# A graph network kernel: the first layer's preparation reordered, and the second layer's chunk checks moved into the first layer's loop

## The chip, the core and the metric

The kernel runs on one core of a Trainium2 chip. The metric is the device time of one execution in microseconds (us), the median of several runs. Engines are named as in the profile: PE is the matrix engine (its weight loads are listed as PEld), DVE the vector engine, ACT the scalar engine, POOL the GpSimd engine, and SP the engine that only issues DMAs. A small q behind a name (SPq, ACTq, POOLq) means the part of that engine that issues DMAs and waits.

## What is computed

Two message passing layers run over one graph with 6250 nodes of 64 features and 200000 edges. The edges are sorted by target (`dst`). `src` and `dst` are integers, and every edge has 64 features of its own.

```python
h = relu(layernorm(x))
# layer 0: a graph convolution with degree norm
deg = segment_sum(1, dst) + 1; dis = rsqrt(deg)
h0 = h @ W
agg = segment_sum(h0[src] * (dis[src] * dis[dst])[:, None], dst) + h0 * (dis * dis)[:, None]
x = x + (h + gelu(agg + b))
h = relu(layernorm(x))
# layer 1: a message network over [h[src], h[dst], edge_attr]
m = relu(concat(h[src], h[dst], edge_attr) @ mW1 + mb1) @ mW2 + mb2
agg = segment_sum(m, dst)
x = x + relu(concat(agg, h) @ uW1 + ub1) @ uW2 + ub2
```

## The kernel before

The order of PE, DVE, ACT and SP is written out by hand in the first two stages (of POOL too in the first): an engine executes its instructions in the order in which the code issues them. There are three stages one after the other.

**The preparation** (`pre`) loads the node features, `src` and `dst`, and builds what the first layer needs. Its steps are these.
- `runs` holds `dst` as 125 rows of 1600. DVE compares every hundredth target with the blocks' limits, PE counts, and `at_run_i` says in which run of 100 each block of nodes begins. POOL gathers those runs (13 indirect DMAs at L392), and `begin` (L423 to L427) finds in them where each group of four nodes begins (`gstart`).
- POOL gathers 192 targets and 192 sources for each of 13 blocks of groups (`gdst`, then `gsrc`, L451).
- `offsets` turns `gdst` on DVE into offsets in the group. `sums` (65 times on ACT, L473) sums them for the degrees. `keys` (L516 to L558) turns a pair of blocks into the low bits of the sources, which go to DRAM through one of two buffers `lows`, and into `key_a` and `key_b`, which PE transposes (`pk`) and ACT and DVE copy out of PSUM.
- `feature_major` transposes the normed features into `hT` in groups of four tiles (PE, then an ACT copy). From the degrees comes `dis`; `gs_block` (PE `ph` L201, DVE L203) makes the scaled features in seven parts, and two casts on ACT and two subtractions on DVE split each part into three bf16 terms `hs`.
- `dstd` and `srcd` are the second layer's "chunk" edges (119 chunks of 1024 edges, 8 per partition), loaded in pieces of 32 bytes. From `dstd` DVE computes, for the second layer, `base`, `off`, `sel`, `nsel`, `ends` and a few checks (`third`, `want`, `more`). `dstb` and `srcb` are the edges of 22 "sections" (28 per partition), from which come `bits`, `hib` and checks of the same kind.
- A table of +1 and -1 (`nbit`, `own`, `table`) is built on DVE at the start.

**The first layer** is a loop over 196 "quads" (49 tiles of sources with four quads each). In a quad PE recodes low bits into a one-hot form (`bank` L893), ACT applies a threshold (`cl` L896), DVE makes one-hot keys (`cka` eight times, `ckb` four times, L907), PE multiplies the two into counts (`pc` L913), ACT or DVE copies the counts out (`a` L918), and PE multiplies the counts with `hs` (`small` L932). A `cka` or `ckb` lies in one of a ring of buffers: DVE can make the next only when PE has finished with the oldest.

```python
ok = cw.tile([P, m], BF16, name=name, bufs=12 if e < 2 else 6)
nc.vector.tensor_scalar(ok, iota_k[:, :m], key[:, col : col + 1], None,
                        op0=ALU.is_equal)
```

Between the quads, by a list of events (`at(n, engine, f)`), 22 sections of the second layer's edges are put into place. A section `s` begins at quad `s * 190 / 22`: DVE `mark` in the same quad, PE `before` (28 matmuls, L783) one quad later, ACT `carry` (L787) two later, then DVE `scan` (L791) three, `place` (L798 to L806) four and `codes` (L814 to L821) five quads later. Edge features are loaded by SP, transposed and multiplied on PE (`turn`, `term`), copied by ACT, and POOL scatters 28 x 128 rows per section to DRAM (L851). Every seven tiles a group of nodes is finished (`node_steps`).

**The second layer** then works through 119 chunks and 22 sections, and takes over half of the time. The diff does not touch its code.

Of the kernel before, what the change touches and what calls it, by code (L numbers as in the profile page):

```python
# [22 lines left out]
J = 8  # L23
# [14 lines left out]
def kernel(  # L38
# [103 lines left out]
    def tail(v):  # L142
        return v[TAIL:E].rearrange("(p j) -> p j", j=J)
# [40 lines left out]
    upper_b = kp.tile([P, P], BF16, name="upper_b")  # L184

# [21 lines left out]
    with tc.tile_pool(name="pre", bufs=1) as pre, \  # L207
# [10 lines left out]
        dstd = pre.tile([P, CD, J], I32, name="dstd")  # L218
        nc.sync.dma_start(dstd[:, : CD - 1, :], edges(dst, 0, CD - 1, EB))
        nc.sync.dma_start(dstd[:, CD - 1, :], tail(dst))  # L220
# [35 lines left out]

        ident = const.tile([P, P], F32, name="ident")
# [18 lines left out]
        top = pre.tile([P, P], F32, name="top")  # L276
        nc.gpsimd.memset(top, 0.0)
        nc.gpsimd.memset(top[:1], 1.0)
        want = pre.tile([P, NS + CD], F32, name="want")
# [8 lines left out]
        for i in range(2):  # L288
            t = pre.tile([P, 2, KS, GS], BF16, name=f"lows{i}")
            nc.gpsimd.memset(t[:, :, KS - 1, :], 1.0)  # L290
            lows.append(t)
# [19 lines left out]
        ident_h = const.tile([P, P], F16, name="ident_h")  # L311
# [22 lines left out]


        nbit = pre.tile([P, KS, P], I32, name="nbit")
        for k in range(KS - 1):
            nc.vector.tensor_scalar(nbit[:, k, :], num, k, 1, op0=ALU.arith_shift_right,
                                    op1=ALU.bitwise_and)
        nc.vector.tensor_tensor(nbit[:, KS - 1, :], num, ti[:, 1:2].to_broadcast([P, P]),  # L340
                                ALU.arith_shift_right)
        nc.vector.tensor_scalar(nbit[:, KS - 1, :], nbit[:, KS - 1, :], 1, None,
                                op0=ALU.bitwise_and)
        own = pre.tile([P, 2, P], F32, name="own")
        nc.vector.tensor_reduce(own[:, 0, :], nbit[:, : KS - 1, :].rearrange("p k n -> p n k"),
                                AX.X, ALU.add)
        nc.vector.tensor_scalar(tf[:, 3:], tf[:, :1], float(KS - 1), None, op0=ALU.is_equal)
        nc.vector.tensor_scalar(own[:, 0, :], own[:, 0, :], -2.0, float(KS), op0=ALU.mult,
                                op1=ALU.add)
        nc.vector.tensor_scalar(own[:, 0, :], own[:, 0, :], tf[:, 3:], None, op0=ALU.mult)  # L350
        nc.vector.tensor_scalar(own[:, 1, :], nbit[:, KS - 1, :], 2.0, -1.0, op0=ALU.mult,
                                op1=ALU.add)
        nc.vector.tensor_add(own[:, 0, :], own[:, 0, :], own[:, 1, :])
        pair = pre.tile([P, PW], F32, name="pair")
        nc.vector.tensor_scalar(pair, iota[:, :PW], tf[:, 1:2], None, op0=ALU.is_equal)
        nc.vector.tensor_tensor(table, own[:, :1, :].to_broadcast([P, PW, P]),
                                pair[:, :, None].to_broadcast([P, PW, P]), ALU.mult)

# [32 lines left out]
        for b in range(NB):  # L391
# [5 lines left out]
        lead = pre.tile([P, NS + CD], F32, name="lead")  # L397
        nc.vector.tensor_copy(lead[:, :NS], dstb[:, :, 0])
        nc.vector.tensor_copy(lead[:, NS:], dstd[:, :, 0])
        pbase = few(NS + CD)  # L400
        nc.tensor.matmul(pbase, top, lead, start=True, stop=True)
        base = pre.tile([P, NS + CD], F32, name="base")
        nc.vector.tensor_copy(base, pbase)
        nc.vector.tensor_scalar(at_i, base[:1], float(NP - P), 0.0, op0=ALU.min, op1=ALU.max)
        off, offb = dstd.bitcast(F32), dstb.bitcast(F32)
        nc.vector.tensor_tensor(off, dstd, base[:, NS:, None].to_broadcast([P, CD, J]), ALU.subtract)
        nc.vector.tensor_tensor(offb, dstb, base[:, :NS, None].to_broadcast([P, NS, SJ]),
                                ALU.subtract)
        nc.vector.tensor_copy(bits[:, :, :, 1], offb)
        nc.vector.tensor_scalar(bits[:, :, :, 0], srcb, P - 1, None, op0=ALU.bitwise_and)  # L410
        nc.vector.tensor_scalar(srcb, srcb, 7, None, op0=ALU.arith_shift_right)
        nc.vector.tensor_copy(hib, srcb)


# [5 lines left out]
        def begin(b0_, n):  # L420
# [9 lines left out]
        begin(*begins[0])  # L430


        nc.vector.tensor_tensor(sel, off, off[:, :, 0:1].to_broadcast([P, CD, J]), ALU.not_equal)
        third = pre.tile([P, CD, J], BF16, name="third")
        nc.vector.tensor_tensor(third, off, off[:, :, J - 1 : J].to_broadcast([P, CD, J]),
                                ALU.not_equal)
        begin(*begins[1])
        nc.vector.tensor_mul(third, third, sel)
        more = pre.tile([P, 7], F32, name="more")
        nc.vector.tensor_tensor(want, base, want, ALU.is_lt)  # L440
        nc.vector.tensor_reduce(more[:, 5:6], want, AX.X, ALU.max)
        begin(*begins[2])
        nc.vector.tensor_tensor(most, base[:, :NS], most, ALU.is_gt)
        nc.vector.tensor_reduce(more[:, 6:], most, AX.X, ALU.max)
        nc.vector.tensor_reduce(more[:, 4:5], third.rearrange("p c j -> p (c j)"), AX.X, ALU.max)
        begin(*begins[3])
        for b in begins[4:]:
            begin(*b)
# [28 lines left out]
        mean = pre.tile([P, Q], F32, name="mean")  # L477
        nc.vector.tensor_reduce(mean, xs, AX.X, ALU.add)
        nc.vector.tensor_scalar(mean, mean, 1.0 / D, None, op0=ALU.mult)
        offsets(*pairs[0])  # L480
        sums(*pairs[0])
        xc = pre.tile([P, Q, D], F32, name="xc")
        nc.vector.tensor_tensor(xc, xs, mean[:, :, None].to_broadcast([P, Q, D]), ALU.subtract)
# [28 lines left out]
        def keys(b0_, n):  # L512
# [5 lines left out]
            lo = lows[b0_ // 2 % 2]  # L518
# [27 lines left out]
            for i, to in enumerate((key_a, key_b)):  # L546
# [3 lines left out]
                if i < 1:  # L550
                    nc.scalar.copy(to[:, b0_ * P : (b0_ + n) * P],
                                   pk[:, :n].rearrange("p b g -> p (b g)"))
                else:
                    pkv = pk[:, :n].rearrange("p b (g two) -> p (b g) two", two=2)
                    c = slice(b0_ * P // 2, (b0_ + n) * P // 2)
                    for e in range(2):
                        r = slice(64 * e, 64 * e + 64)
                        nc.vector.tensor_copy(to[r, c], pkv[r, :, e])  # L558

        quads = blocks(4)  # L560
        for q in quads[:4]:
            feature_major(*q)
        sums(*pairs[5])
        keys(*pairs[0])
        for q in quads[4:8]:
            feature_major(*q)
        sums(*pairs[6])
        keys(*pairs[1])
        for q in quads[8:]:
            feature_major(*q)  # L570
# [7 lines left out]
        keys(*pairs[2])  # L578
# [18 lines left out]
        keys(*pairs[3])  # L597

        gs = xc
        for i, (q, n) in enumerate(blocks(8)):  # L600
            s = slice(q, q + n)
            gs_block(psum, gs, q, n)
            nc.scalar.copy(hs[:, s, 0, :], gs[:, s])
            if i < 3:
                keys(*pairs[4 + i])
            nc.vector.tensor_sub(gs[:, s], gs[:, s], hs[:, s, 0, :])
            nc.scalar.copy(hs[:, s, 1, :], gs[:, s])
            if i:
                nc.vector.tensor_sub(hs[:, last, 2, :], gs[:, last], hs[:, last, 1, :])
            last = s  # L610
        nc.vector.tensor_sub(hs[:, last, 2, :], gs[:, last], hs[:, last, 1, :])

        for i, v in enumerate((off.rearrange("p c j -> p (c j)"),
                               offb.rearrange("p s j -> p (s j)"))):
            nc.vector.tensor_reduce(more[:, i : i + 1], v, AX.X, ALU.max)
            nc.vector.tensor_reduce(more[:, 2 + i : 3 + i], v, AX.X, ALU.min)
        nc.vector.tensor_scalar(more[:, :2], more[:, :2], float(P), None, op0=ALU.is_ge)
        nc.vector.tensor_scalar(more[:, 2:4], more[:, 2:4], 0.0, None, op0=ALU.is_lt)
        nc.vector.tensor_reduce(flag[:, NS:], more, AX.X, ALU.max)
        nc.vector.tensor_reduce(nsel, sel, AX.X, ALU.add)  # L620
        for i in range(2):
            nc.vector.tensor_copy(ends[:, i], off[:, :, i * (J - 1)])

        nc.vector.memset(ends[:DDONE, :, CD - 1], -1.0)
# [126 lines left out]
    def section_events(pool, psum, at, pace, placed):  # L751
# [107 lines left out]
        for s in range(NS):  # L859
            o = Section(s)  # L860
            n0 = s * pace
            at(n0, "dve", o.mark)
            at(n0 + 1, "pe", o.before)
            at(n0 + 2, "act", o.carry)
            at(n0 + 3, "dve", o.scan)
            at(n0 + 4, "dve", o.place)
            at(n0 + 5, "dve", o.codes)
            for b in range(Q // 7):
                at(n0 + b, "sp", lambda s=s, b=b: clear(s + 2, b))
            for j0, n in blocks(J, SJ):  # L870
                m = n0 + 3 + j0 * pace / SJ
                for d, engine, f in ((-4, "sp", o.load), (0, "pe", o.turn), (1, "act", o.turned),
                                     (2, "pe", o.term), (3, "act", o.put)):
# [4 lines left out]
    with tc.If(is_bad < 1) as branch:  # L878

        with tc.tile_pool(name="cw", bufs=2) as cw, tc.tile_pool(name="cn", bufs=1) as cn, \  # L880
# [17 lines left out]
            def count(n, i, a, ol):  # L898
                w, q = divmod(n, NQD)
                pc = psum.tile([P, 2, 512], F32, name="pc")  # L900
                for u in range(2):
                    pr = w * PW + q * QP + i + u
                    for e in range(3):
                        key, col, m, name = ((key_a, 2 * pr + e, KA, "cka") if e < 2 else
                                             (key_b, pr, KB, "ckb"))
                        ok = cw.tile([P, m], BF16, name=name, bufs=12 if e < 2 else 6)
# [48 lines left out]

            here, events = [0], {}
# [520 lines left out]
```

## Time and profile before

| | us |
|---|---|
| median of three runs (2473.94 to 2478.30) | 2474.47 |
| the profiled execution | 2476.56 |
| its span from first to last instruction | 2474.80 |
| of it: preparation, up to the first `cb` load | 158 |
| of it: the first layer, up to the second layer's steady work | 945 |
| of it: the second layer | 1372 |

Engine time inside the three stretches (busy us, from the windows view):

| stretch | PE | DVE | ACT | POOL | granted PE clock |
|---|---|---|---|---|---|
| 0 to 158 | 42.8 | 108.1 | 51.7 | 57.8 | 0.80 |
| 158 to 1103 | 845.3 | 798.2 | 728.5 | 693.0 | 0.94 |
| 1103 to 2475 | 1174.9 | 1010.4 | 873.8 | 958.8 | 0.88 |

A group of the profile is a line, an engine and an operation with what it writes and reads; then come the count, the busy time and the mean duration of one in ns, and behind the second bar the time that the engine sat idle just before them and who ended that idle time. A line of the waits view is a waiting engine and line, what it waited for, the total, the number of times, and the longest. A line of the timeline is start, duration, engine, line, operation and shapes, with the idle time before it in brackets. The windows view has, after the stretch, the busy time of PE, PEld, DVE, ACT and POOL, the granted clock of PE as a share of full speed, the DMA share and GB/s.

### The profile page before, as it was taken

What the parts mean: (1) busy time and instruction counts of PE and PEld (TensorE: products, weight loads), DVE (VectorE), ACT (ScalarE), POOL (GpSimd) and SP (SyncE); (2) the same over time, 40 slices, a digit from 0 to 9 for tenths busy, and PEclk for the clock granted to TensorE, in tenths of its full rate; (3) what the DMA queues carried; (4) which work ended last, traced back from release to release, by engine and by line L of the source; (5) the groups of instructions that cost most, each with busy time, mean ns of one, the idle gap of its engine ahead of it and who ended that gap; (6) DMA issues with size and microseconds to landing.
All of it is one profiled execution on the core that took longest, in us unless ns stands there. A gap on an engine that the chain in (4) does not pass through costs nothing.

```text
span 2474.8 us, 50145 instructions
## 1 busy us (share of the span) xinstructions
PE 2062.9 (83%) x17607; PEld 1740.3 (70%) x17607; DVE 1916.7 (77%) x6239; ACT 1653.9 (67%) x3773; POOL 1709.6 (69%) x1676
## 2 busy tenths in 40 slices
PE   0369999998989998858888888888888888888887
PEld 0247777776767776647777777777777778777775
DVE  7678989888887988747768776776677787767875
ACT  0648787877778887746666665665567576656664
POOL 6307777777777777757777777777667677767770
PEclk9769999999999998977889998998889898989997
DMA  9423323332323231133333332233223232322210
GB/s 149 88 68 103 100 95 109 98 105 93 103 90 105 90 120 54 41 82 90 79 75 83 96 84 75 77 79 78 69 76 79 62 85 75 81 72 80 76 50 9
DMA packets 216156, 205.47 MB, mean 83 GB/s; under 512 B 118369, under 2 KB 166369, under 8 KB 215886
## 3 DMA queue, kind: packets, MB, share of 16 engines
q1 hardware_dynamic: 140258, 141.92, 20.6%
q0 software_dynamic: 51840, 57.23, 9.1%
q10 hardware_dynamic: 23788, 2.94, 1.2%
q8 instruction: 143, 2.34, 0.4%
q14 instruction: 127, 1.04, 0.1%
HBM read 133.66 MB, written 68.28 MB: 82 GB/s over the span
## 4 chain that ended last, share of the span: by engine, by line
PE 32%; ACT 13%; DVE 5%; DMA 3%; issue 2%; POOL 2%; SPq 0%; DVEq 0%; ACTq 0%; POOLq 0%
PE duo L1346 9%; PE pz L1328 6%; ACT oh L1320 5%; ACT h L1193 4%; PE pl L1316 3%; PE pp L1179 3%; PE pl L1204 2%; POOL g L746 2%; PE pz L1332 2%; PE mix L1182 2%; ACT hid L1339 1%; DMA g<-table,srcd 1%; PE pe L1160 1%; ACT h L1191 1%; PE mix L1170 1%
## 5 line engine op out<-in xcount | busy, mean ns | idle before, releaser
L746 POOL DMA_INDIRECT g<-table,srcd x952 | 972.2, 1021 | 347.1 <-issue 247.0
L851 POOL DMA_INDIRECT sorted<-rows,to x616 | 675.8, 1097 | 230.0 <-issue 159.6
L1320 ACT ACTIVATE oh<-pl,six 128x480 bf16<-128x480 f32 x616 | 352.9, 606 | 141.3 <-PE pl L1316 134.9
L896 ACT ACTIVATE cl<-bank,six 128x512 bf16<-128x512 f32 x588 | 394.5, 714 | 22.2 <-PE bank L893 13.1
L907 DVE TENSOR_SCALAR cka<-iota_k,key_a 128x196 bf16<-128x196 f16 x1568 | 375.8, 290 | 6.1 <-PE pc L913 6.0
L913 PEld LDWEIGHTS <-cl 128*128 128x128 bf16 x2352 | 218.2, 99 | 216.3 <-issue 92.5
L1328 PEld LDWEIGHTS <-oh 128*120 128x120 bf16 x2156 | 280.2, 146 | 117.6 <-issue 77.2
L1342 DVE TENSOR_SCALAR ms<-iota,es 120x128 f32<-120x128 f32 x1078 | 264.8, 301 | 108.9 <-PE duo L1346 105.4
L1346 PE MATMUL duo<-hid,ms 120*128 120x65 f32 x2156 | 289.6, 290 | 40.8 <-ACT hid L1339 38.7
L913 PE MATMUL pc<-cka,cl 128*128 128x196 bf16 x1568 | 271.5, 252 | 61.3 <-DVE cka L907 59.1
L918 ACT CAST a<-pc 128x784 bf16<-128x784 f32 x343 | 287.7, 839 | 47.8 <-PE pc L913 47.5
L1346 PEld LDWEIGHTS duo<-hid,ms 120*128 120x128 f32 x2156 | 272.1, 204 | 56.1 <-ACT hid L1339 53.1
L1332 PEld LDWEIGHTS <-oh 128*120 128x120 bf16 x2156 | 279.2, 147 | 15.2 <-issue 5.0
L1328 PE MATMUL pz<-bs,oh 128*120 128x128 bf16 x1078 | 247.9, 261 | 22.7 <-ACT oh L1320 21.5
L913 PE MATMUL pc<-ckb,cl 128*128 128x392 bf16 x784 | 263.9, 337 | 3.2 <-ACT cl L896 1.8
L1328 PE MATMUL pz<-ts,oh 128*120 128x128 bf16 x1078 | 259.1, 253 | 1.5 <-DVE zs L1337 1.2
L907 DVE TENSOR_SCALAR ckb<-iota_k,key_b 128x392 bf16<-128x392 f16 x784 | 259.3, 331 | 0.0
L1316 PE MATMUL pl<-ct,code 98*128 98x480 bf16 x616 | 205.9, 369 | 54.2 <-ACT oh L1320 50.6
L932 PE MATMUL small<-hs,a 128*128 128x192 bf16 x2401 | 244.1, 255 | 0.0
L1193 ACT ACTIVATE h<-z,sel 128x64 f32<-128x64 f32 x952 | 239.5, 338 | 0.0
L932 PEld LDWEIGHTS <-a 128*128 128x128 bf16 x2401 | 214.4, 101 | 21.3 <-issue 5.4
L893 PE MATMUL bank<-table,cb 128*128 128x512 bf16 x588 | 204.7, 392 | 18.4 <-DVE cka L907 8.4
(303 smaller groups left out, 4151.5 us busy)
## 6 DMA issues: line engine op xcount, KB each, us to landing
ea<-in_edge_attr_dram SPq DMA_DIRECT2D x185, 256.0 KB
sorted<-zero SPq DMA_DIRECT2D x154, 236.2 KB
es<-sorted SPq DMA_DIRECT2D x154, 236.2 KB
g<-table,srcd POOLq DMA_INDIRECT x952
sorted<-rows,to POOLq DMA_INDIRECT x616
cb<-bits SPq DMA_DIRECT2D x49, 96.0 KB
bits<-lows SPq DMA_DIRECT2D x26, 128.0 KB
ea<-in_edge_attr_dram SPq DMA_DIRECT2D x22, 128.0 KB
```

The source lines that it names most:

```text
L746: nc.gpsimd.indirect_dma_start(out=g[:, j, :], out_offset=None, in_=table[:, :], in_offset=bass.IndirectOffsetOnAxis(ap=srci[:, c, j : j + ...
L851: put = nc.gpsimd.indirect_dma_start(out=sorted_[self.s][:, :], in_=self.rows[:, j, :], in_offset=None, out_offset=bass.IndirectOffsetOnAx ...
L896: nc.scalar.activation(ol[:, e].rearrange("p i n -> p (i n)"), pl, AF.Relu, bias=six)
L907: nc.vector.tensor_scalar(ok, iota_k[:, :m], key[:, col : col + 1], None, op0=ALU.is_equal)
L913: nc.tensor.matmul(to, ol[:, e, i + u, :], ok, start=(e == 0), stop=(e == 2), skip_group_check=True)
L918: copy(a[:, :, c : c + 4 * G].rearrange("p h (u t) -> p u h t", u=2), pc[:, :, :KB].rearrange("p u (h t) -> p u h t", t=2 * G))
L932: nc.tensor.matmul(pg, as_[w][:, h, :], hs[:, h].rearrange("p k d -> p (k d)"), start=False, stop=(h == Q - 1), skip_group_check=True)
L1193: nc.scalar.activation(h[:, 1, j], z[:, j], AF.Relu, scale=sel[:, c, j : j + 1])
L1320: nc.scalar.activation(oh[:, t, g : g + n, :], pl[:, :n], AF.Relu, bias=six)
L1328: nc.tensor.matmul(pz[:CAP, g - g0].rearrange("p i d -> p (i d)"), oh[:, t, g, :], v[:, :2].rearrange("p i d -> p (i d)"), start=(t == 0), ...
L1332: nc.tensor.matmul(pz[:CAP, g - g0, 0, :], oh[:, t, g, :], v[:, 2, :], start=False, stop=(t == 1), skip_group_check=True)
L1346: nc.tensor.matmul(pa, m[:CAP, g, :], h[:CAP, g, :], start=(k == 0 and g == 0), stop=(k == NG - 1 and g == NG - 1), skip_group_check=True)
```

## The change

- `dstd` is no longer loaded in the preparation. SP loads `runs` and then `dstb` and `srcb`.
- The table's DVE steps (`nbit`, `own`, `table`) move from the start to between the `begin` steps; `mean` and `xc` move up there too.
- In ACT's order all `sums` come before the first copy of `feature_major`; the copies of `key_b` out of PSUM move from DVE to ACT.
- `lows` has three buffers, not two. `keys` of pairs 2 and 3 move from before the loop over the parts into it: five pairs are now among the seven parts, and the subtractions of a part come one and two parts later.
- What is computed from `dstb` and `srcb` moves to the end of the preparation.
- What is computed from `dstd` moves into the first layer's events (`chunk_events`): the load at quad 24, the first target's base at quads 36 to 38, and eleven DVE steps at every second quad from 40 to 60.
- The first section's events are pulled together into quads 0 and 1, and its edge loads and scatters come up to four quads sooner.
- The rings of `cka` and `ckb` have 8 and 4 buffers, not 12 and 6.

```diff
-        dstd = pre.tile([P, CD, J], I32, name="dstd")
-        nc.sync.dma_start(dstd[:, : CD - 1, :], edges(dst, 0, CD - 1, EB))
-        nc.sync.dma_start(dstd[:, CD - 1, :], tail(dst))
...
-        for i in range(2):
+        for i in range(3):
             t = pre.tile([P, 2, KS, GS], BF16, name=f"lows{i}")
...
-        nbit = pre.tile([P, KS, P], I32, name="nbit")
...
-        lead = pre.tile([P, NS + CD], F32, name="lead")
-        nc.vector.tensor_copy(lead[:, :NS], dstb[:, :, 0])
...
         begins = blocks(3, NB)
+        nbit = pre.tile([P, KS, P], I32, name="nbit")
...
         begin(*begins[0])
-        nc.vector.tensor_tensor(sel, off, off[:, :, 0:1].to_broadcast([P, CD, J]), ALU.not_equal)
...
+        own = pre.tile([P, 2, P], F32, name="own")
...
         begin(*begins[1])
+        nc.vector.tensor_reduce(mean, xs, AX.X, ALU.add)
...
         begin(*begins[2])
         begin(*begins[3])
+        begin(*begins[4])
+        nc.vector.tensor_tensor(xc, xs, mean[:, :, None].to_broadcast([P, Q, D]), ALU.subtract)
...
                     for e in range(2):
                         r = slice(64 * e, 64 * e + 64)
-                        nc.vector.tensor_copy(to[r, c], pkv[r, :, e])
+                        nc.scalar.copy(to[r, c], pkv[r, :, e])
 
         quads = blocks(4)
-        for q in quads[:4]:
+        sums(*pairs[5])
+        sums(*pairs[6])
+        for q in quads[:5]:
             feature_major(*q)
-        sums(*pairs[5])
         keys(*pairs[0])
...
-        keys(*pairs[2])
...
-        keys(*pairs[3])
...
+        parts = [slice(q, q + n) for q, n in blocks(8)]
+        for i in range(len(parts) + 2):
+            if i < len(parts):
+                q = parts[i]
+                gs_block(psum, gs, q.start, q.stop - q.start)
+                nc.scalar.copy(hs[:, q, 0, :], gs[:, q])
+            if i < 5:
+                keys(*pairs[2 + i])
+            if 0 < i <= len(parts):
+                q = parts[i - 1]
+                nc.vector.tensor_sub(gs[:, q], gs[:, q], hs[:, q, 0, :])
+                nc.scalar.copy(hs[:, q, 1, :], gs[:, q])
+            if i > 1:
+                q = parts[i - 2]
+                nc.vector.tensor_sub(hs[:, q, 2, :], gs[:, q], hs[:, q, 1, :])
+        lead = pre.tile([P, NS], F32, name="lead")
...
             n0 = s * pace
+            a = [0, 0, 1, 1, 1, 1] if s == 0 else list(range(6))
+            for d, engine, f in zip(a, ("dve", "pe", "act", "dve", "dve", "dve"),
+                                    (o.mark, o.before, o.carry, o.scan, o.place, o.codes)):
+                at(n0 + d, engine, f)
...
-                m = n0 + 3 + j0 * pace / SJ
+                m = n0 + (3 if s else 0) + j0 * pace / SJ
...
-                        ok = cw.tile([P, m], BF16, name=name, bufs=12 if e < 2 else 6)
+                        ok = cw.tile([P, m], BF16, name=name, bufs=8 if e < 2 else 4)
...
+            def chunk_events(n0):
+                dstd = cn.tile([P, CD, J], I32, name="dstd")
+                off = dstd.bitcast(F32)
+                lead = cn.tile([P, CD], F32, name="lead")
...
+                at(n0, "sp", load)
+                at(n0 + 12, "dve", lambda: nc.vector.tensor_copy(lead, dstd[:, :, 0]))
+                at(n0 + 12, "pe", least)
+                at(n0 + 14, "dve", base)
+                for i, f in enumerate((
+                        lambda: nc.vector.tensor_tensor(
+                            off, dstd, lead[:, :, None].to_broadcast([P, CD, J]), ALU.subtract),
+                        lambda: nc.vector.tensor_tensor(
+                            sel, off, off[:, :, 0:1].to_broadcast([P, CD, J]), ALU.not_equal),
+                        *[lambda i=i: third(i) for i in range(4)],
+                        lambda: nc.vector.tensor_reduce(more[:, 0:1], flat, AX.X, ALU.max),
+                        lambda: nc.vector.tensor_reduce(more[:, 2:3], flat, AX.X, ALU.min),
+                        lambda: nc.vector.tensor_reduce(nsel, sel, AX.X, ALU.add),
+                        last, all_)):
+                    at(n0 + 16 + 2 * i, "dve", f)
...
                 section_events(cw, psum, at, (NQUADS - 6) / NS, put)
+                chunk_events(24)
```

`third(i)` does, for a quarter of the chunks, one comparison, one product and one maximum; `last` makes two copies into `ends`, a small memset and one maximum; `all_` combines the checks.

## The prediction

> **What bounds the kernel now.** I read the windows view first (table above), then the waits of preparation and first layer, then the timeline. No engine fills the preparation's 158 us, so a chain sets its end:
>
> ```profile
> ACT L473 <- DMA gdst<-in_dst_dram,gstart: 49.4, 1, 49.4
> ...
> DVE lead L398 <- DMA dstb<-in_dst_dram: 13.5, 1, 13.5
> ```
> ```profile
> 45.40 1.60 POOL L451 DMA_INDIRECT gdst<-in_dst_dram,gstart  x1 [2.88 <-DVE gstart L427]
> ```
> ```profile
> 59.49 0.46 ACT L473 ACTIVATE over<-gdst,less 128x192 bf16<-128x192 f32 x1 [7.93 <-DVE gdst L467]
> ```
> ```profile
> 116.34 0.69 DVE L203 TENSOR_TENSOR xc<-ph,dis 128x512 f32<-128x512 f32 x1 [3.01 <-PE ph L201]
> ...
> 125.16 0.69 DVE L203 TENSOR_TENSOR xc<-ph,dis 128x512 f32<-128x512 f32 x1 [2.29 <-PE ph L201]
> ```
>
> DVE stands 13.5 us for `dstb`; POOL cannot gather targets before 45.4, so ACT's sums start at 59.5. Later DVE and PE take turns: 8.82 us from one `gs_block` product to the next, as PE runs `ph` (3.67 us for eight tiles) only behind the transposes of `keys`.
>
> The first layer is different. PE is busy 845 of 945 us, and its largest wait is for DVE's one-hots:
>
> ```profile
> PE pc L913 <- DVE cka L907: 59.1, 34, 4.8
> ...
> DVE upto L791 <- ACT has L787: 44.7, 20, 3.7
> ...
> DVE cka L907 <- PE pc L913: 5.6, 8, 2.1
> ```
>
> The timeline of one section shows why (DVE first, then PE):
>
> ```profile
> 324.60 3.12 DVE L791 TENSOR_TENSOR_SCAN upto<-run,has 128x1421 bf16<-128x1421 bf16 x1 [1.02 <-ACT has L787]
> 327.63 0.43 DVE L907 TENSOR_SCALAR cka<-iota_k,key_a 128x196 bf16<-128x196 f16 x2
> ...
> 330.94 2.51 DVE L800 TENSOR_REDUCE place<-upto 128x28 f32<-128x1372 bf16 x1
> ```
> ```profile
> 327.27 0.59 PE L893 MATMUL bank<-table,cb 128*128 128x512 bf16 x2
> ...
> 330.71 0.59 PE L893 MATMUL bank<-table,cb 128*128 128x512 bf16 x2
> ...
> 335.05 0.42 PE L913 MATMUL pc<-cka,cl 128*128 128x196 bf16 x2 [2.62 <-DVE cka L907]
> ```
>
> I counted in the timeline, at each scan, the `cka` that DVE had made less the `pc` matmuls on `cka` that had ended. At 21 of 22 scans it is 12, the whole ring (once 9). During the scan's 3.12 us it falls to about 4; `place` takes another 4.7 us; then the ring is empty and PE waits about 2 us. The ring is what PE lives on while DVE serves a section.
>
> **The change, part by part.** All sums are against the profiled execution, 2476.56 us (span 2474.80), which lies 2.1 us above the median.
>
> *Rings of 8 and 4: +36 us.* With 8 buffers DVE reaches each scan 8 ahead instead of 12; nothing in scan, `place` or `codes` gets shorter. So PE runs dry four `cka` sooner, which is half a quad. From `bank` at 327.27 to 330.71 a quad takes PE 3.44 us: half is 1.7 us, times 21 sections, 36 us. With the sections' own matmuls a quad takes (901 - 59) / 196 = 4.3 us (quads run from 161 to 1062): 2.1 us and 45 us at most. Less than 36 is possible if DVE's wait for `has` (44.7 us in all) is now spent sooner and PE finds work in between; I keep 15 as the low end. I take 36, because the rows beside the waits have 3.44 us.
>
> *Chunk checks in the loop: +7 us.* DVE gets, by the rows of the same shapes: cast 0.43, base, clamp and `want` 0.8, `off` 1.13, `sel` 1.14, the quarters of `third` 1.14 + 1.14 + 1.13 plus some 0.8 for twelve starts, maximum and minimum 1.14 each, `nsel` 1.13, `ends` 0.5, the small ones 0.8: 12.4 us over 24 quads. The first step waits for the load, twelve quads after its issue, which is long enough. Queued behind each on DVE are `cka`s, and PE waits for those. Bounds: 0 if all fall where DVE stands with a full ring, 12.4 if none does. A third of all `cka` (540 of 1568, same count) start 8 or more ahead, where DVE will have to stand anyway; two thirds of 12.4 are 8, and I take 7, as DVE also stands for `has` and `a`. PE's one matmul (0.81 us at L401) is in that.
>
> *The load of `dstd` at quad 24: +1 us.* Its 15,232 packets of 32 bytes held SP's next issue 26.75 us in the preparation (L220). Behind it on SP are `cb`, edge features, clears and stores. The next `cb` is issued four quads (18 us) later and needed seven quads (30 us) after the load, edge features likewise, so the queue is free in time; without this slack it costs up to 9 us. POOL's scatters share the DMA engines, which are 0.33 busy there. I take 1, bounds 0 and 9.
>
> *First section sooner: +1 us.* Scan, `place` and `codes` (9 us) fall together into quad 1, where DVE has little lead; before, PE waited 3.8 us at 177.6 for the first one. POOL starts sooner, but the last rows come at a fixed quad. Bounds -2 and +4.
>
> *Preparation: -5 us.* Its steps:
> - `runs` lands when its last 6400-byte packet ends, at 11.5 by the trace's DMA records; DVE reached it at 17.54 behind the table. Now DVE (free at 5.9) takes it at 11.8, 5.7 sooner, and `at_run_i` is ready at 18.7 (6.86 us later, as before).
> - POOL's 13 gathers of runs take 17.8 (24.69 to 42.52), to 36.8; `begin` is done in between, so `gdst` starts at 36.8 (before 45.40). The wait for `dstb` is gone; what is late next is POOL's own order.
> - Two gathers and their landing end by 42, but DVE has table (5), five `begin` (1.3 each), `mean` (3.6) and `xc` (3.4) ahead of the first `offsets`: 45. ACT's sums start at 45.7, 13.8 sooner.
> - All sums, `Square` and `std` are 33 us of ACT: 78.6. Then 13 `hT` copies (0.8 each with PE's part), and two pairs' DMA issues, `key_a` and two `key_b` copies (2.3 each): 93.8. The degrees' matmuls and `dis` take 3.0: 96.3, against 108.2.
> - But `keys` 2 and 3 now come after that, each inside a turn. `ph` 2.8, four turns of 8.82, a single-block turn of 7.5, 4 us of last subtractions: 145.9 (before 152.3).
> - Then what is computed from `dstb`: 7.2 us (1.5 for `lead` and its matmul, 3.3 for L404 to L412, 1.6 maximum and minimum, 0.8 small), against 5.6 of checks before: 153.1, against 157.9.
>
> The third `lows` buffer takes a wait away that the trace does not show: 0. `key_b` on ACT: two copies (0.3 each) wait there for PE's `pk`, and behind them stand the casts `hs`, for which only subtractions wait, and these lie beside `ph` (DVE idles 2.3 to 3.0 us there): 0; without that cover 0.6 us per turn, 3 in all. Bounds for the preparation: 0 (all eaten by `keys`) and -14 (all of ACT's lead kept).
>
> A rule is weighed here. The granted clock stood at half while `ph` ran 10.93 us without a gap (137.73 to 148.66):
>
> ```profile
> 140.00:150.00 10.00, 8.90 (x42) 8.59 (x41) 5.02 (x8) 3.09 (x5) 0.00 (x0) 0.50 0.00 1
> ```
>
> The Trainium skill ("TensorE: Matmul & The Clock Gate", Part 1) says that some 3.4 us of sustained matmuls bring the full clock; by it, each of the five turns would lose about half of `ph`, 1.8 us, the preparation would gain 14 and the sum would be +31. The trace does not agree, and I go by the row: half clock, 3.67 us.
>
> Sum: 36 + 7 + 1 + 1 - 5 = +40: 2516.6 for the profiled execution, 2514.5 for the median, say 2514. The second layer's 1372 us stay.
>
> **Rivals.**
> *Faster: ACT's lead reaches the end.* The preparation hangs on POOL and ACT up to 99; if the turns of PE and DVE pack tighter than 8.82 us, all 13.8 us are kept. For it: DVE idles 2 to 3 us per turn. Against it: PE is what DVE waits for, and two more pairs enter the turns. It decides only if rings, checks, load and first section together cost less than 13.8 us, which needs the rings to cost under 0.3 us per section; the wait for `has` (44.7 us) would have to show that the last four buffers were never needed. Then -10: 2464.
> *No change.* The rings cost the low end, 15, the checks little, and all of ACT's lead is kept: 15 + 1 - 14 is about 2476.
> *Much slower: the load collides.* If SP stays blocked 27 us and the 15,232 packets also hold up scatters and edge features, 9 us come on top; with checks at 12.4 and rings at 45: 45 + 12 + 9 + 4 - 5 = +65, 2540.
> *The change does not do what it says:* in the built program's order the moves are there, and DVE's first wait on PE for a `cka` stands at the ninth, so I give this nothing.
>
> **How the numbers follow.** This kernel can be told from no change at about 0.2% (5 us). Forecast 0.70, much slower 0.12, faster 0.13, no change 0.05. So slower 0.82, same 0.05, faster 0.13. The forecast's own range is 2490 (rings 20, checks 3, preparation -9) to 2530 (rings 45, checks 12). Leaving out the faster rival and no more than some tail, the range is 2484 to 2540.
>
> **What would show it.** Right: `pc` on PE waits for `cka` some 95 us in place of 59, two to four times per section still; `cka` waits for PE far more than 5.6 us, and the wait of the scan for `has` nearly vanishes; no scan starts more than 8 ahead; `gdst` is gathered from 37, sums from 46, first `cb` load at about 153; quads 1 to 195 take some 945 us in place of 901. Wrong: the quads take about 900 us, or the preparation ends before 145. If the quads at 36 to 60 alone lengthen, the checks and not the rings were the price; if a single gap of 10 us stands at quads 24 to 32, it was the load.

## The result, and the profile after

The changed kernel takes 2504.77 us (median of four runs, 2500.18 to 2517.90), the kernel before 2476.39 us (four runs, 2473.94 to 2482.34). The ratio is 1.012, with an interval of 1.0074 to 1.0165: slower by 28 us. The profiled execution of the changed kernel took 2508.9 us (span 2507.14, granted clock 0.896), 32.3 us more than the one before.

Stages of the two profiled executions, from the trace (us). A quad begins with the first of its three thresholds `cl` on ACT.

| | before | after | difference |
|---|---|---|---|
| preparation, to the end of `upper_b` | 157.9 | 145.4 | -12.5 |
| quads 0 to 12 | 49.0 | 51.5 | +2.5 |
| quads 12 to 36 | 107.7 | 111.4 | +3.7 |
| quads 36 to 62 | 117.8 | 131.3 | +13.5 |
| quads 62 to 195 | 626.0 | 640.1 | +14.1 |
| second layer, from its first gather | 1389.2 | 1400.7 | +11.5 |

The waits of the changed kernel's first layer (waiting engine and line; what for; total us, times, longest):

```profile
DVE cka L881 <- PE pc L887: 123.0, 81, 6.4
...
PE pc L887 <- DVE cka L881: 83.6, 48, 7.6
```

PE's wait for one-hots grew by 24.5 us. DVE's wait for a free buffer went from almost nothing to 123.0 us, and its wait for `has` is no longer in the list. Its wait for the counts that it copies to `a`, 56.2 us before (28 times), is nearly gone too:

```profile
DVE a L892 <- PE pc L887: 4.7, 12, 1.7
```

DVE's three waits sum to 106.9 us before (6.0 + 44.7 + 56.2 over the first layer) and to 127.7 us after. So DVE did not come to stand 123 us more; most of its standing moved from `has` and `a` to the ring, and 21 us are new.

One section in the timeline (DVE, then PE), to be held against the one shown before:

```profile
656.59 0.45 DVE L881 TENSOR_SCALAR cka<-iota_k,key_a 128x196 bf16<-128x196 f16 x2 [2.71 <-PE pc L887]
...
657.78 3.12 DVE L766 TENSOR_TENSOR_SCAN upto<-run,has 128x1421 bf16<-128x1421 bf16 x1
...
664.09 2.50 DVE L775 TENSOR_REDUCE place<-upto 128x28 f32<-128x1372 bf16 x1
```
```profile
653.45 2.59 PE L758 MATMUL bank<-has,upper_b 128*128 128x49 bf16 x28
...
656.31 0.33 PE L887 MATMUL pc<-cka,cl 128*128 128x196 bf16 x2
...
661.11 0.42 PE L887 MATMUL pc<-cka,cl 128*128 128x196 bf16 x2 [0.56 <-DVE cka L881]
...
667.66 0.42 PE L887 MATMUL pc<-cka,cl 128*128 128x196 bf16 x2 [2.48 <-DVE cka L881]
```

DVE stands 2.71 us for a buffer just ahead of the scan, and then starts it with five `cka` ready instead of 12. The two orders show why. The ring is full while PE works on the 28 matmuls of `before`, and four more `cka` stand ahead of the scan in DVE's order. When PE is back at `pc`, it uses seven `cka` in 1.4 us, in which DVE makes those four; so it is at 20 of the 21 scans behind the first (seven or eight used, four made). With 12 buffers DVE had made them by then and stood for `has` (20 times, 44.7 us). PE is dry already at the end of the scan (0.56 us, new), and again at the end of `place` (2.48 us, where before it was 2.62). Over all sections I summed PE's gaps ahead of `pc` by their place: at the end of the scan 0.3 us before (once) and 15.1 us after (16 times); at the end of `place` 43.7 and 53.7; elsewhere 18.8 and 18.4. The price of a section is thus mostly a second, short stop.

The preparation, in the order of its chain:

```profile
36.91 0.95 POOL L423 DMA_INDIRECT gdst<-in_dst_dram,gstart  x1 [0.30 <-DMA runs<-in_dst_dram,at_run_i]
...
45.96 0.45 ACT L445 ACTIVATE over<-gdst,less 128x192 bf16<-128x192 f32 x1 [3.09 <-DVE gdst L439]
```
```profile
92.73 0.69 DVE L206 TENSOR_TENSOR xc<-ph,dis 128x512 f32<-128x512 f32 x1 [1.05 <-PE ph L204]
...
101.55 0.69 DVE L206 TENSOR_TENSOR xc<-ph,dis 128x512 f32<-128x512 f32 x1 [4.10 <-PE ph L204]
```

POOL gathers targets 8.5 us sooner, ACT sums 13.5 us sooner, the first `gs_block` product comes 23.6 us sooner. The turns still take 8.82 us, and there are more of them with `keys` inside; of the 23.6 us, 12.5 are left at the end of the preparation.

### The profile page after: what moved, and what is told of

Read it like the earlier page. It is cut to its first block, busy times and chain, and to the rows that moved or that the text cites. A ratio compares the mean times of both kernels' runs of the same rounds, so it can differ in the third digit from the quotient of the medians.

```text
span 2507.1 us, 50182 instructions
## 1 busy us (share of the span) xinstructions
PE 2078.8 (83%) x17609; PEld 1749.8 (70%) x17609; DVE 1908.9 (76%) x6237; ACT 1660.4 (66%) x3787; POOL 1710.9 (68%) x1677
## 4 chain that ended last, share of the span: by engine, by line
PE 31%; ACT 13%; DVE 5%; DMA 3%; issue 3%; POOL 2%; SPq 0%; DVEq 0%; ACTq 0%; POOLq 0%
PE duo L1384 9%; PE pz L1366 6%; ACT oh L1358 5%; ACT h L1231 4%; PE pl L1354 3%; PE pp L1217 2%; PE pl L1242 2%; POOL g L721 2%; PE pz L1370 2%; DMA g<-table,srcd 2%; PE mix L1220 2%; ACT hid L1377 1%; PE pe L1198 1%; ACT h L1229 1%; DVE z L1222 1%
## 5 line engine op out<-in xcount | busy, mean ns | idle before, releaser
L881 DVE TENSOR_SCALAR cka<-iota_k,key_a 128x196 bf16<-128x196 f16 x1568 | 365.8, 288 | 123.4 <-PE pc L887 123.0
L887 PEld LDWEIGHTS <-cl 128*128 128x128 bf16 x2352 | 216.4, 98 | 247.8 <-issue 105.9
L1366 PEld LDWEIGHTS <-oh 128*120 128x120 bf16 x2156 | 285.3, 148 | 119.2 <-issue 78.5
L1370 PEld LDWEIGHTS <-oh 128*120 128x120 bf16 x2156 | 284.7, 150 | 15.3 <-issue 5.1
L1370 PE MATMUL pz<-ts,oh 128*120 128x64 bf16 x1078 | 217.4, 204 | 0.0
```

What stands on the lines that cost most here:

```text
L887: nc.tensor.matmul(to, ol[:, e, i + u, :], ok, start=(e == 0), stop=(e == 2), skip_group_check=True)
L1366: nc.tensor.matmul(pz[:CAP, g - g0].rearrange("p i d -> p (i d)"), oh[:, t, g, :], v[:, :2].rearrange("p i d -> p (i d)"), start=(t == 0), ...
L1370: nc.tensor.matmul(pz[:CAP, g - g0, 0, :], oh[:, t, g, :], v[:, 2, :], start=False, stop=(t == 1), skip_group_check=True)
```

## Experiments

The profiles above were taken at a mean granted clock of 0.90. The twelve runs of this section fell on three chips that granted 0.71 to 0.74, and the kernel before took 3554 to 3647 us there; they are called the slower chips below. More than the clock differs: over a whole profile DVE and ACT each stand some 400 to 600 us there for releases that the waits view calls `remote`, because it finds no recorded instruction for them; the two profiles at 0.90 have none. So each time is compared with the kernel before on the same chip, as a ratio, and a profile of these chips only with others of these chips. What they tell of sizes is the price on those chips.

**The rings alone, from both sides.** In the kernel before, smaller rings (on two chips) and larger ones:

```diff
-                        ok = cw.tile([P, m], BF16, name=name, bufs=12 if e < 2 else 6)
+                        ok = cw.tile([P, m], BF16, name=name, bufs=8 if e < 2 else 4)
```

> The kernel before with one line changed: rings of 8 and 4 buffers for `cka` and `ckb`. Theory A (the rings are what the first layer pays): quads 911 us (first `bank` matmul to last `small` matmul) become some 938 to 945, PE's wait for `cka` grows from 59 to about 85 us, the wait of the scan for `has` (44.7) falls to almost nothing; time about 2505. Theory B (the rings are slack, because DVE spends the wait for `has` in them; the checks, the load and the first section cost the 34 us): quads stay within 5 us of 911, time 2476 to 2482. The preparation stays at 157.9 in both.

> The first four runs fell on a chip that granted PE a clock of 0.71 to 0.73 (before: 0.89), and the kernel before took 3647 us there: PE alone set the pace and the rings could not show. The same edit again, rings of 8 and 4 in the kernel before, with the same question, for a chip at the clock of the first profiles (0.89). Theory A: quads 911 us become 938 to 945, PE's wait for `cka` some 85 us, time about 2505. Theory B: quads within 5 us of 911, time 2476 to 2482.

Measured: ratio 1.0011 (0.9971 to 1.0050) and 1.0068 (1.0038 to 1.0098), so 4 to 25 us: the first cannot be told from no change, the second is on the side of theory A, with a price below the one it named for the faster clock. How far the quads grew cannot be said exactly, as the kernel before has no profile on these chips; the nearest is the run with larger rings below, on another of them, whose quads 0 to 195 take 1192 us, against 1216 with the small rings on the second chip (the same kernel's quads differ by 3 to 21 us between two of these chips, in the pairs below). The waits of DVE with these rings, on the second chip:

```profile
DVE cka L907 <- PE pc L913: 191.0, 121, 6.1
...
DVE a L918 <- PE pc L913: 23.3, 14, 3.9
```

> The kernel before with rings of 14 and 7 buffers: the same price from the other side. If each buffer that DVE can be ahead is worth the same as in A (34 us for four), two more bring 10 to 17 us: quads 895 to 900, time 2460 to 2466. If DVE's lead is bounded by its own time and not by the ring (rival), nothing moves: quads 908 to 911, time 2473 to 2477.

Measured: ratio 0.9975 (0.9942 to 1.0009), not distinguishable from no change. That speaks for the rival, but the interval leaves room for the 10 to 17 us; the profile is what decides. Its waits of DVE:

```profile
DVE a L918 <- PE pc L913: 84.9, 20, 12.9
DVE cka L907 <- PE pc L913: 58.0, 44, 3.8
DVE upto L791 <- ACT has L787: 48.5, 16, 5.3
```

With 14 buffers DVE still starts 18 of the 22 scans 12 ahead: what stops it there is `has`, not the ring. With 8 it never waits for `has`. The same swap as in the changed kernel comes from this one line, so the swap is shown to be the rings' doing. PE's gaps show it too: at the end of the scans they are 9.3 us with the small rings and 0.6 with the large, at the end of `place` 37.5 against 27.4. That is 19 us at those two places, the two at which the changed kernel lost 25.

**The changed kernel with the large rings.** They do not fit beside the new tiles; so `dstd` is loaded into the memory of `sel`, each quarter makes its own comparison with the first target, and `sel` itself is computed behind them.

```diff
-                        ok = cw.tile([P, m], BF16, name=name, bufs=8 if e < 2 else 4)
+                        ok = cw.tile([P, m], BF16, name=name, bufs=12 if e < 2 else 6)
...
-                dstd = cn.tile([P, CD, J], I32, name="dstd")
-                off = dstd.bitcast(F32)
+                off, dstd = sel, sel.bitcast(I32)
...
```

> The changed kernel with rings of 12 and 6 buffers again. To make room for them, `dstd` is loaded into the memory of `sel` and worked on in place, and each quarter compares with the first target by itself (four DVE steps of some 0.3 us more). Theory A: quads come back to 915 to 920 (911 and what the checks, the load and the first section cost), the preparation stays at 145, so the time is about 2466 to 2472, faster than both kernels. Theory B: quads stay near 945, time near 2500. Theory C (the second layer took part of the loss, as the profile of after has 1400.7 us from its first gather where before has 1389.2): even with quads back near 915, the time stays near 2478.

> The changed kernel with rings of 12 and 6 (`dstd` in the memory of `sel`) again, for a chip at a clock of 0.89. Theory A: quads 915 to 920, preparation 145, time 2466 to 2472. Theory B: quads near 945, time near 2500. Theory C (second layer): quads near 915, time near 2478.

Measured: ratio 1.0007 (0.9977 to 1.0038) and 1.0032 (1.0000 to 1.0064). Against the changed kernel (1.0072, below) the rings bring some 0.4 to 0.65%, or 14 to 23 us of 3600, though the intervals overlap, and not the speed that I expected: something else still cost about what the preparation gained. Theory C finds no support here, but its 11 us could not be seen either: from the last quad to the end the profiles of these chips take 2224 to 2294 us.

**The first section's events.** Both with large rings (on two chips) and with the rings of the changed kernel:

```diff
-            a = [0, 0, 1, 1, 1, 1] if s == 0 else list(range(6))
+            a = list(range(6))
...
-                m = n0 + (3 if s else 0) + j0 * pace / SJ
+                m = n0 + 3 + j0 * pace / SJ
...
-                                     (2 if s else 1, "pe", o.term), (3 if s else 2, "act", o.put)):
+                                     (2, "pe", o.term), (3, "act", o.put)):
```

> As the changed kernel with rings of 12 and 6 (and `dstd` in the memory of `sel`), with the first section's events where the kernel before has them. The prediction put the earlier first section at +1 us (bounds -2 and +4): so this run should be 1 us shorter than the run with the earlier section, by the first 12 quads, and at most 4 us shorter or 2 us longer. PE's wait of 7.6 us at the first section should go back to some 4 us.

> As the one with rings of 12 and 6, with the first section's events where the kernel before has them, for a chip at a clock of 0.89. By the prediction (+1, bounds -2 and +4, for the earlier section) 1 us shorter than with the earlier section. On the slow chip it was 25 us shorter in the median, which the first 12 quads cannot account for if the section costs 1 us; if that difference comes back here, the earlier first section has a price that I did not see; if it is under 5 us, the 25 us were that chip's scatter.

> The changed kernel, rings of 8 and 4, with only the first section's events put back to where the kernel before has them. In the two pairs of runs with rings of 12 and 6 this brought 0.7% (some 24 us at a clock of 0.72), of which the profiles show 15 us in quads 0 to 12; in the first profile of the changed kernel, at 0.90, these quads are only 2.5 us longer than before. If the earlier section costs as much with the small rings: quads 0 to 12 fall from 68 to 60 us, the ratio to before from 1.007 to 1.000 (0.997 to 1.003). If the price hung on the large rings: ratio 1.004 to 1.009.

Measured: 0.9937 (0.9905 to 0.9969) and 0.9961 (0.9927 to 0.9996) with large rings, 0.7% below the same kernels with the early section, on both chips; 1.0043 (1.0002 to 1.0083) with small rings, 0.3% below the changed kernel on another chip, which its interval does not tell from nothing. Quads 0 to 12 take 60.2 and 59.1 us instead of 75.5 and 74.1 (large rings), and 60.9 instead of 68.5 (small). But with small rings the next quads give it back:

| us, slower chips | quads 0 to 12 | 12 to 36 | 0 to 36 |
|---|---|---|---|
| changed, large rings, early section | 75.5 and 74.1 | 145.3 and 146.2 | 220.8 and 220.3 |
| changed, large rings, late section | 60.2 and 59.1 | 146.6 and 149.7 | 206.8 and 208.8 |
| changed, small rings, early section | 68.5 | 147.9 | 216.4 |
| changed, small rings, late section | 60.9 | 156.9 | 217.8 |
| before (late section), small rings, second chip | 62.3 | 159.6 | 221.9 |
| before (late section), rings of 14 and 7 | 59.0 | 146.7 | 205.7 |

The two runs on the preparation below have small rings and the early section too, on the chip of the late one; their quads 0 to 36 take 217.3 and 218.6 us. So on these chips the early first section costs 11 to 14 us with large rings, which the prediction did not have, and nothing that shows by quad 36 with the small rings of the change: only large rings and a late section together make these quads short. Of the two answers that were set for the last run, the second is the one that fits: the price hangs on the large rings. The remaining 10 us of the 0.7% have no place that I found. The version with large rings and the late section, run on two chips, is the only one faster than the kernel before; on these chips it beats the changed kernel by 1.1 to 1.35%. At a clock of 0.90 it was not run.

That the early section can cost more than its steps is seen in the windows of the changed kernel at clock 0.90 (behind the stretch: PE, PEld, DVE, ACT and POOL busy; the granted clock):

```profile
156.40:164.00 7.60, 0.05 (x1) 0.00 (x0) 7.36 (x12) 1.81 (x3) 0.00 (x0) 0.82 0.38 120
164.00:168.10 4.10, 4.09 (x18) 3.06 (x18) 3.32 (x17) 1.61 (x3) 0.00 (x0) 0.51 0.00 0
168.10:172.10 4.00, 3.80 (x30) 2.58 (x28) 3.66 (x18) 4.00 (x8) 3.06 (x3) 1.00 0.24 61
```

Scan, `place` and `codes` stand together, PE stops for 7.56 us, and then works at half clock for 4.1 us (a `pc` of 128x392 takes 0.53 us, afterwards 0.33). The Trainium skill ("TensorE: Matmul & The Clock Gate", Part 1) says that an idle window of some 3.4 us drops the clock to half and a busy one brings it back. These rows agree with both halves. The turns of the preparation do not show the second half: PE is busy 22.2 of 46.9 us, in runs of up to 4.6 us, and the clock stays at half, as it did in the prediction's row through 10.93 us of `ph` without a gap; there the measurement decides:

```profile
92.70:139.60 46.90, 22.16 (x100) 19.11 (x100) 30.20 (x102) 12.13 (x29) 0.00 (x0) 0.50 0.38 76
```

Slower work makes only 1 to 2 of the 11 to 14 us on the slower chips: with large rings PE is busy 49.8 and 49.1 us in quads 0 to 12 with the early section, 48.6 and 47.5 with the late one. The rest is standing: 7.6 us at the section, as at 0.90, and then above all a second stop of 9.6 and 7.3 us for ACT's copy `eT`. Why ACT is late there stays open.

**The changed kernel again, and its chunk steps twice.**

```diff
                     at(n0 + 16 + 2 * i, "dve", f)
+                    if 0 < i < 9:
+                        at(n0 + 17 + 2 * i, "dve", f)
```

> The changed kernel itself once more, as the measure for the next run and for the seven before, which all fell on chips that granted 0.71 to 0.73. At a clock of 0.89: time 2500 to 2518 and quads (first to last `bank`) near 934 by the records of ACT's thresholds; its second layer shows whether the 11 us that the first profile of it had over the kernel before there come back (theory C) or were scatter. At a clock near 0.72: by theory A the rings cost less there, since PE is slower and DVE is not, so the change costs less than 1.2%: between 0 and 0.8%; by theory B (checks, load, first section), as much as before or more.

> The changed kernel with eight of the eleven chunk steps (`sel`, the four of `third`, maximum, minimum, `nsel`) issued a second time one quad later: 8.75 us more for DVE between quads 42 and 58, with the same results. In the profiles of before and after, quads 36 to 62 grew by 13.4 us, where the other quads from 12 on grew by 0.11 us each; so I now read the checks as some 10 us, not 7. If so, these quads grow by another 6 to 8 us over the changed kernel, and nothing else does. Rival (the checks lie where DVE stands anyway, and the growth there is the smaller rings): under 2 us.

Measured: ratio 1.0072 (1.0028 to 1.0117) for the changed kernel, 1.0075 (1.0036 to 1.0114) with the steps twice. Up to quad 36 the two profiles run alike (216.4 and 216.2 us); quads 36 to 62 take 157.2 and 162.2 us: 5.0 us for 9.4 us more on DVE. But quads 62 to 195, where nothing differs, drifted by 9.1 us, some 0.07 us per quad, which would be 1.8 us of the 5.0; and the three other profiles with small rings and the steps once have 156.9 to 159.9 us in quads 36 to 62, so that 2 to 5 us are left. The kernel before with small rings, without any of these steps there, has 158.6 on the second chip, no less than the changed kernel. So on these chips the price of the checks does not stand out from the scatter, and the second issue of the steps cost about half of its DVE time at most.

**Two parts of the preparation.** `keys` of pairs 2 and 3 ahead of the loop, and the last two `sums` between the copies:

```diff
+        keys(*pairs[2])
         cnt = pre.tile([P, G, NB], F32, name="cnt")
...
+        keys(*pairs[3])
         gs = xc
...
-            if i < 5:
-                keys(*pairs[2 + i])
+            if i < 3:
+                keys(*pairs[4 + i])
```

> The changed kernel with `keys` of pairs 2 and 3 before the loop over the parts again, three pairs in the loop. The prediction charged 5.5 us for the two pairs inside the turns (49.6 us from `dis` to the last subtraction, 44.1 before). By it, the stretch from `dis` to the last subtraction is some 4 to 5.5 us shorter than in the changed kernel, and `dis` comes 3 us later: the preparation ends 1 to 2.5 us sooner. Rival: a turn takes 8.82 us with or without keys, because PE and DVE wait for each other anyway; then the stretch keeps its length and the preparation ends 3 us later.

```diff
-        sums(*pairs[5])
-        sums(*pairs[6])
-        for q in quads[:5]:
+        for q in quads[:4]:
             feature_major(*q)
+        sums(*pairs[5])
         keys(*pairs[0])
-        for q in quads[5:9]:
+        for q in quads[4:8]:
             feature_major(*q)
+        sums(*pairs[6])
```

> The changed kernel with the last two `sums` between the `hT` copies again (four groups, sums, keys, four groups, sums, keys, the rest), as before. Working of the prediction: ACT does the same work in another order, so `dis` moves by less than 1 us; what the change gained, it gained by earlier targets. Rival: with all sums first, copies that wait for PE's transposes no longer hold sums back; then `dis` comes 2 to 5 us later here, and the preparation ends as much later.

Both have one profile each and are compared with the run of the first section on the same chip, whose preparation is that of the changed kernel (in the seven profiles that have this preparation it ends between 148.7 and 150.2 us):

| us | changed | keys ahead | sums between |
|---|---|---|---|
| `dis` ready | 93.3 | 94.9 | 94.5 |
| from there to the last subtraction | 49.6 | 44.2 | 49.6 |
| end of the preparation | 148.7 | 144.9 | 149.9 |

The products on DVE, keys inside (first fence) and ahead (second):

```profile
113.64 0.69 DVE L206 TENSOR_TENSOR xc<-ph,dis 128x512 f32<-128x512 f32 x1 [3.49 <-PE ph L204]
...
122.45 0.69 DVE L206 TENSOR_TENSOR xc<-ph,dis 128x512 f32<-128x512 f32 x1 [2.89 <-PE ph L204]
...
131.27 0.69 DVE L206 TENSOR_TENSOR xc<-ph,dis 128x512 f32<-128x512 f32 x1 [2.89 <-PE ph L204]
```
```profile
120.69 0.69 DVE L206 TENSOR_TENSOR xc<-ph,dis 128x512 f32<-128x512 f32 x1 [3.49 <-PE ph L204]
...
128.15 0.69 DVE L206 TENSOR_TENSOR xc<-ph,dis 128x512 f32<-128x512 f32 x1 [2.78 <-PE ph L204]
...
131.56 0.69 DVE L206 TENSOR_TENSOR xc<-ph,dis 128x512 f32<-128x512 f32 x1 [1.52 <-PE ph L204]
```

A turn with `keys` takes 8.82 us, a turn without 3.41 us. Two turns less bring 5.4 us, as the prediction had charged, and the two pairs cost only 1.6 us ahead of `dis`: that part of the change loses 3.8 us, more than the 1 to 2.5 us expected. With sums between the copies the preparation ends 1.2 us later, within the spread of the others, and 0.5 us of it are there before the first sum; so the order of ACT is not what made the preparation shorter. That the earlier targets are follows from the chain above, and was not tried alone. The version that the runs point to is the changed preparation with `keys` 2 and 3 ahead, large rings and the late first section; this combination was not run.

## Why the prediction held, and which terms were off

The forecast said 2514, slower; the time is 2505, and the mechanism is the one it named: PE runs dry in the sections because DVE has fewer one-hots ready. But two terms of its sum, the rings and the preparation, were mis-sized in the same direction, together by some 21 us, and the second layer, which it had left alone, took 11.5 us more. Without the second layer's part the profiled execution would have been 21 us slower, half of the +40. That the total came as near as it did is in part luck.

- *Rings, +36.* Outside of quads 0 to 12 and 36 to 62 the loop grew by 17.8 us in 157 quads (3.7 + 14.1), or 0.113 per quad, so 22 us in all 196. Of the 17.8 us, 14.9 are PE standing. DVE's new standing, 21 us, is of the same size. The step that failed is "four `cka` sooner, half a quad, at each section", and it failed twice. DVE does not arrive 8 ahead but 4 or 5 (at 21 of 22 scans; once 8): PE uses up seven or eight in the time in which it makes the last four ahead of the scan. That speaks for a higher price. Yet DVE no longer stands 44.7 us for `has` and 51.5 us for `a`: what it now stands for the ring, it stood for these before. The low end of 15 was there for this reason; the likeliest value should have weighed it.
- *Checks, +7.* Quads 36 to 62 grew by 13.5, of which the rings' rate takes 2.9: 10.6 us, for 12.5 us of DVE's time. But only 6.2 of the 13.5 us are PE standing. In the other 7.2 it is busy longer with the same matmuls, at a granted clock of 0.95 instead of 0.99 (before, then after):

```profile
318.23:436.07 117.84, 110.35 (x967) 88.75 (x965) 105.88 (x376) 95.62 (x159) 92.24 (x85) 0.99 0.33 101
```
```profile
311.40:442.69 131.29, 117.56 (x963) 92.34 (x961) 117.55 (x408) 96.36 (x159) 96.44 (x87) 0.95 0.30 92
```

  Less the rings' share of the standing (14.9 us in 157 quads, so 2.5 here, an estimate) the checks made PE stand some 4 us; whether they also lowered the clock is not shown. Their price lies between 4 and 11 us. The bounds of 0 and 12.4 hold both.
- *Load, +1.* Quads 24 to 36 grew by 0.9 us, less than the rings' rate makes (1.4): nothing is left for the load.
- *First section, +1.* Quads 0 to 12 grew by 2.5, of which the rings' rate makes 1.4: about 1, as predicted, at clock 0.90. On the slower chips it was 11 to 14 with large rings, beyond the upper bound of 4, and with the small rings of the change nothing that shows by quad 36.
- *Preparation, -5.* It was -12.5, near the end of the range (-14). Up to the end of the sums each step came within 0.6 us of the prediction (`runs` taken at 12.4, `gdst` 36.9, sums 46.0 to 78.8). Then four terms were too dear. The last copy ended at 90.4 instead of 93.8: the first five took 0.80 us each, as in the row that the prediction used, but the next four 0.59 and the last four, one of them short, 0.51, and what stands between the groups took 3.2 us instead of 4.6. `dis` came 1.2 us after the last copy, not 3.0 (the prediction's sum is off by a little here: 78.6, 10.4 and 4.6 make 93.6, not 93.8, and with 3.0 that is 96.6, not 96.3). The stretch to the last subtraction was 47.9, not 49.6, as the first product started 1.1 us after `dis`, not 2.8. The tail behind it took 5.8, not 7.2.
- *Second layer, 0.* The profile has 11.5 us more. By ACT's `h` of each chunk the two executions stay within 5.2 us of each other up to chunk 91; from chunk 95 to the last one the difference goes from -2.0 to +11.5. It is work that takes longer, and no waiting: PE was busy 12.1 us longer with the same 10,310 matmuls, at a mean granted clock of 0.87 instead of 0.88 (before, then after):

```profile
1085.60:2474.80 1389.20, 1180.41 (x10310) 1037.28 (x10310) 1019.46 (x3169) 877.83 (x2407) 973.65 (x957) 0.88 0.29 75
```
```profile
1106.40:2507.10 1400.70, 1192.53 (x10310) 1050.54 (x10310) 1020.95 (x3169) 878.87 (x2407) 972.03 (x957) 0.87 0.29 75
```

The four times of the changed kernel spread by 18 us, and the difference of the medians is 28.4 us where the two profiles have 32.3. So a part of the 11.5 us may be the scatter of one execution. Whether the change makes any of it stays open: all later runs were on the slower chips.

Of the signs that the forecast named, six came: the wait of the scan for `has` gone, `cka` waiting far more, no scan over 8 ahead, two stops of PE per section, `gdst` at 37, sums at 46. The quads took 934 us, not 945, PE waited 84 us for `cka`, not 95, and the preparation ended at 145.4, not 153.1, just above the 145 that was named as a sign of being wrong. The faster rival asked for rings under 0.3 us per section; they cost 1.0 us (22 us over 22 sections). The load did not collide. The rival of no change had rings at 15 and the whole of ACT's lead kept; it was right about the preparation and short by 7 on the rings and by 4 to 10 on the checks.

## What to carry to other kernels

A ring's depth is worth what its user can refill between two interruptions, less what that user then loses at other waits: before a shorter ring is priced by its buffers, add up the waits that the longer ring only moved (here 96 us of DVE's standing, for `has` and `a`). Work that is moved into a loop has to be priced with what makes room for it: here the smaller rings paid for the memory of the moved tiles, and the two together cost more than the preparation gained.

## What the runs showed of the hardware that was not expected

- After a stop of 7.56 us PE worked at a granted clock of 0.51 for 4.1 us and then at 1.00; that adds about 2 us to the stop itself (an estimate, half of the 4.1). In the turns of the preparation the clock stayed at 0.50 throughout, also through 10.93 us of `ph` without a gap.
- The kernel before took 2476 us at a mean granted clock of 0.90 and 3554 to 3647 us on the chips that granted 0.71 to 0.74. There its preparation (157.4 to 157.7 us in the runs with other rings, instead of 157.9) hardly noticed, that of the changed kernel took 3 to 5 us more (148.7 to 150.2 instead of 145.4), and the quads of the versions run there took 1192 to 1225 us. The second layer took 2224 to 2294 us where it took 1413 and 1424 at 0.90 (all from the last quad on), some 1.6 times as long at a granted clock of 0.62 to 0.65 instead of 0.86 to 0.88: more than the granted clock accounts for.
- Prices changed with the chip: the early first section, worth about 1 us at 0.90, cost 11 to 14 us on the slower chips, but with large rings alone.
